# Third stage of a four-layer convolution net: group statistics back to rows through TensorE in two 12-bit halves, residual shared anew

## The chip, the cores and the metric

The kernel runs on one core of one Trainium2 chip. The metric is the time of one execution on the device in microseconds (us), the median of several runs. Inputs are random normal numbers of 8192 x 8 x 16 x 16 in float32.

## The reference, cut to what matters

Four layers, each with its input normalised by groups (four groups of two channels, over all pixels of a group of one sample) and added to its output:

```
def _gn(v, G=4, eps=1e-5):          # per sample and group: (g - mean) / sqrt(var + eps)
x = x + tensor_train_matvec(_gn(x)) + bias                 # layer 0
x = x + relu(batchnorm(conv3x3(_gn(x)) + bias))            # layer 1: statistics over the whole batch
x = x + conv3x3(round(clip(_gn(x) * sx)), qw) / (sx * sw) + bias   # layer 2: sx = 127 / max|_gn(x)|, over the whole batch
x = x + conv3x3(pad_edge(_gn(x)), sign(w) * mean|w|) + bias        # layer 3
```

The two maxima and averages over the whole batch cut the program into three stages. The third does layers 2 and 3, and the change is in it.

## The kernel before, in words

The batch is cut into 64 tiles of 128 samples. In the third stage a tile is an array of 128 partitions (channel and image row) by 2048 columns (sample and image column). A convolution along the rows and channels is a product with a band matrix of 128 x 128; the three taps along the columns are three products that add up in PSUM. A normalisation needs its group's mean and 1/sigma for each sample. Sums come out of TensorE with samples spread over the rows; to be used, they must lie along the columns again, the same in all partitions of a group ("rows").

Each step of a tile is a small function, and the table OPS names it. For tile i:

- "rows2", "spread2": 1/sigma times sx of the layer-2 normalisation, which stage 2 left in gnst as columns, is spread by DVE over a diagonal pattern (to_rows) and transposed by DVE in blocks of 32; TensorE then copies it to all partitions by a product with the selection matrix sel0, into r2 (bank ps_a).
- "v", "q": DVE multiplies the tile by r2 and rounds to int8, ACT turns it into bf16. "c2h1", "c2h0": layer 2's products, one half of the tile each, into pq.
- The residual: for half 0, ACT adds the bias ("bias") and DVE adds pq * inv ("stz", first2). For half 1, ACT makes pq * inv + bias ("z1"), and POOL adds it ("add1").
- "sq", "sums", "small", "pow": ACT squares, TensorE sums (s), DVE reduces and forms mean and variance, POOL takes the power -1/2.
- "rows3", "spread3": mean/sigma, 1/sigma and the mean of layer 2's input go the same way through to_rows, one transpose, and products with sel1 (into r3) and corr (into o3), a matrix that also takes the layer-2 mean out through the convolution's row sums.
- "t", "hi", "lo", "edl": DVE multiplies by r3; ACT and POOL split the product into two parts that float32r holds exactly. "c3h1a" to "c3h0b": layer 3's products into pf. "c", "corr": ACT and POOL add the offset o3. "out1", "out0": DVE adds pf, and SP stores the tile.

The order is written by hand: PHASE gives each step a time within a pipeline, tile i is shifted by PERIOD * i, and the sorted list is the order in which every engine's queue is filled. InOrder keeps that order on PE, DVE, ACT and POOL; a queue never overtakes. pq and pf share one PSUM pool of two buffers (tag "pc"), which rotate in the order in which the steps are written.

Of the kernel before, what the change touches and what calls it, by code (L numbers as in the profile page):

```python
# [8 lines left out]
F32 = mybir.dt.float32  # L9
F32R = mybir.dt.float32r  # L10
# [3 lines left out]
ALU = mybir.AluOpType  # L14
# [18 lines left out]
class InOrder:  # L33
# [5 lines left out]
    def __getattr__(self, name):  # L39
        op = getattr(self.engine, name)  # L40

        def call(*args, **kwargs):
# [2 lines left out]

PERIOD = 11.539
PHASE = {"rows2": 0, "spread2": 0.01, "v": 5.1, "q": 10.2, "bias": 10.4, "c2h1": 11.6, "z1": 13.1, "c2h0": 16.1, "add1": 17.1,
         "stz": 23.1, "sq": 24, "sums": 31.8, "small": 34.7, "pow": 37.3, "rows3": 42.7, "spread3": 45.3, "t": 46.3,  # L50
         "hi": 49.9, "c": 51.2, "lo": 51.9, "corr": 58.8, "edl": 60.3, "c3h0a": 60.4, "c3h0b": 61.3, "out0": 66.8,
         "c3h1a": 69.3, "c3h1b": 69.4, "out1": 69.41}

PACK0 = [("c0", R * C), ("c1", R * H), ("core2", 2 * R * W), ("bias0", W)]
# [5 lines left out]
def tile_net(ctx: ExitStack, tc: tile.TileContext, xb, xt_in, pack0, pack1, pack2, out):  # L62
# [33 lines left out]
    T2 = [dict() for _ in range(NT)]  # L96

    LATE = 5 if NT >= KEEP + STAY + 3 else 0

    def load2(i, what="yx"):  # L100
        for k in what:
# [45 lines left out]
    def late_constants(late):  # L147
# [101 lines left out]
        quarter = L["quarter"] = blocks(32, 1.0, "quarter")  # L249
        gpad = L["gpad"] = const.tile([P, NQ, 32], F32, name="gpad")  # L250
        dve.memset(gpad, 0.0)
        dve.tensor_copy(gpad[:, :, 0:G], quarter.unsqueeze(1).to_broadcast([P, NQ, G]))
        for k, name in enumerate(("sel0", "sel1", "corr")):

            t = L[name] = const.tile([P, CH], F32, name=name)
            dve.tensor_copy(t.rearrange("p (g n) -> p g n", g=G),
                            mod32[:, G * k:G * k + G].unsqueeze(2).to_broadcast([P, G, CH // G]))
        yield "statistics"

    def diagonal(n):  # L260
        ts = []
        for k in range(2):
            t = const.tile([P, NQ, 32], F32, name=f"diag_{n}_{k}")
            nc.gpsimd.memset(t, 0.0)
            ts.append(t)
        return ts
# [8 lines left out]
    def samples(t):  # L275
        return t.rearrange("p (b w) -> p b w", w=W)
# [422 lines left out]
    def put_quarter(ps):  # L699
        nc.vector.tensor_copy(ps[:, 0:NQ], L["quarter"])  # L700

    def stats_small(mv, st, ps, name):

        s = small.tile([P, 32], F32, name=f"s_{name}", tag="s")
        dve.tensor_reduce(s, samples(ps), AX.X, ALU.add)
        dve.transpose(st, s)
        sq = small.tile([P, G], F32, name=f"sq_{name}", tag="sqm")
        dve.tensor_copy(mv[:, 0:G], st[:, 0:G])
        dve.tensor_tensor(sq, st[:, 0:G], mv[:, 0:G], ALU.mult)
        dve.scalar_tensor_tensor(mv[:, G:2 * G], st[:, G:2 * G], EPS, sq, ALU.add, ALU.subtract)  # L710

    def stats_pow(mv):
        pool.tensor_tensor(mv[:, G:2 * G], mv[:, G:2 * G], mhalf[:, :G], ALU.pow)

    def to_rows(diag, mask, cols, name):

        at = 0
        for c in cols:
            n = c.shape[1]
            dve.tensor_tensor(diag[:, :, at:at + n], c.unsqueeze(1).to_broadcast([P, NQ, n]),  # L720
                              mask.unsqueeze(2).to_broadcast([P, NQ, n]), ALU.mult)
            at += n
        rows = small.tile([P, P], F32, name=f"rows_{name}", tag="rows")
        dve.transpose(rows, diag.rearrange("p q j -> p (q j)"))
        return rows
# [6 lines left out]
    with tc.tile_pool(name="p2", bufs=2) as p2, tc.tile_pool(name="ps2", bufs=2, space=PSUM) as ps2:  # L732
# [30 lines left out]

        def stats2(i):

            st, mv = psc[:, 32 + 32 * (i % 2):64 + 32 * (i % 2)], gnst[:, order2[i]]
            red = small.tile([P, 32], F32, name=f"s_c{i}", tag="s")
            dve.tensor_reduce(red, samples(T[i].pop("ps")), AX.X, ALU.add)
            dve.transpose(st, red)
            T[i]["sq"] = small.tile([P, G], F32, name=f"sq_c{i}", tag="sqm")  # L770
            act.copy(mv[:, 0:G], st[:, 0:G])
            act.activation(T[i]["sq"], st[:, 0:G], AF.Square)

        def sigma2(i):
            st, mv = psc[:, 32 + 32 * (i % 2):64 + 32 * (i % 2)], gnst[:, order2[i]]
            dve.scalar_tensor_tensor(mv[:, G:2 * G], st[:, G:2 * G], EPS, T[i].pop("sq"), ALU.add, ALU.subtract)
            stats_pow(mv)

        def spread2(i):
            T[i]["gb"] = ps = ps2.tile([P, BANK], F32, name=f"gb_{i}", tag="gb")  # L780
            rows = to_rows(diag[i % 2], mask2, [gnst[:, order2[i]]], f"c{i}")
            if i % 4 == 0:
                T[i]["gr"] = ps2.tile([P, 4, P], F32, name=f"gr_{i}", tag="gr")
                T[i]["top"] = p2.tile([P, 4, P], F32, name=f"top_{i}", tag="top")
            else:
                T[i]["gr"], T[i]["top"] = T[i - 1]["gr"], T[i - 1]["top"]
            for dst, sel in ((ps[:, 0:P], L["sel0"]), (T[i]["gr"][:, i % 4], L["sel1"])):
                pe.matmul(dst, sel, rows, start=True, stop=True)
# [60 lines left out]
    gm = const.tile([P, 1], F32, name="gm")  # L849
    nc.vector.tensor_reduce(pm, amax, AX.X, ALU.max)  # L850
    nc.gpsimd.partition_all_reduce(gm, pm, P, bass_isa.ReduceOp.max)
    nc.vector.reciprocal(sx, gm)
    nc.vector.tensor_scalar(sx, sx, 127.0, None, ALU.mult)
    nc.vector.tensor_tensor(inv, sx, L["sw"], ALU.mult)
# [6 lines left out]


    with ExitStack() as s:
        wk = s.enter_context(tc.tile_pool(name="wk3", bufs=2))
        ps_c = s.enter_context(tc.tile_pool(name="ps_c3", bufs=2, space=PSUM))
        ps_s = s.enter_context(tc.tile_pool(name="ps_s3", bufs=1, space=PSUM))
        order = [*kept, *(t for t in range(NT) if t not in kept)]

        sq3, t3, z3 = sqs[0], [sqs[1], xh], [y_stay[3][:, h * F // 2:(h + 1) * F // 2] for h in range(2)]
        T = [dict() for _ in range(NT)]  # L870
        AHEAD = min(NT, KEEP - 6)
        diag2, diag3 = diagonal("d"), diagonal("e")

        ps_a, ps_r, ps_o = (ps_s.tile([P, BANK], F32, name=f"ps_{n}", tag=n) for n in ("a", "r", "o"))
        r2, r3, o3 = ps_a[:, 0:P], ps_r[:, 0:P], ps_o[:, 0:P]
        put_quarter(ps_a[:, P:2 * P])
        mask, st3 = ps_a[:, P:P + NQ], ps_a[:, P + 32:P + 64]

        def load3(i):
            t = order[i]  # L880
# [6 lines left out]
        def halves(t):  # L887
            return t.rearrange("p (h n) -> p h n", h=2)

        def rows2(i):  # L890
            T[i]["rows2"] = to_rows(diag2[i % 2], mask, [gnst[:, order[i], G:2 * G]], f"d{i}")

        def rows3(i):
            mv = T[i].pop("mv")
            mr = small.tile([P, G], F32, name=f"mr_{i}", tag="mr")
            dve.tensor_tensor(mr, st3[:, 0:G], mv[:, G:2 * G], ALU.mult)
            T[i]["rows3"] = to_rows(diag3[i % 2], mask, [mr, mv[:, G:2 * G], gnst[:, order[i], 0:G]], f"e{i}")


        def spread2(i):  # L900
            pe.matmul(r2, L["sel0"], T[i].pop("rows2"), start=True, stop=True)

        def spread3(i):
            rows = T[i].pop("rows3")
            pe.matmul(r3, L["sel1"], rows, start=True, stop=True)
            pe.matmul(o3, L["corr"], rows, start=True, stop=True)

        def scale2(i):

# [9 lines left out]
            T[i]["q"] = q  # L919

        def bias2(i):
            x = halves(T[i]["x"])[:, 0]
            act.activation(x, x, AF.Identity, bias=L["bias2"], scale=1.0)

        def layer2(i, h):
# [8 lines left out]
        def first2(i):  # L934
            x = halves(T[i]["x"])[:, 0]
            dve.scalar_tensor_tensor(x, T[i].pop(("pq", 0)), inv, x, ALU.mult, ALU.add)

        def second2(i):
            act.activation(z3[i % 2], T[i].pop(("pq", 1)), AF.Identity, bias=L["bias2"], scale=inv)

        def add2(i):
            x = halves(T[i]["x"])[:, 1]
            pool.tensor_tensor(x, x, z3[i % 2], ALU.add)

        def square3(i):
            act.activation(sq3, T[i]["x"], AF.Square)
# [3 lines left out]
            sums_pe(T[i]["ps"], T[i]["x"], sq3)  # L950

        def stats3(i):
            T[i]["mv"] = small.tile([P, 2 * G], F32, name=f"mv3_{i}", tag="mv")
            stats_small(T[i]["mv"], st3, T[i].pop("ps"), f"d{i}")

        def pow3(i):
            stats_pow(T[i]["mv"])

        def offset3(i):
            T[i]["c"] = small.tile([P, P], F32, name=f"c_{i}", tag="c")  # L960
# [41 lines left out]
        def finish(i, h):  # L1002
# [4 lines left out]
            if T[i]["done"] == 2:  # L1007
                nc.sync.dma_start(out[order[i]], T[i]["x"])
                T[i].clear()

        OPS = {"rows2": rows2, "spread2": spread2, "v": scale2, "q": round2, "bias": bias2,
               "c2h0": lambda i: layer2(i, 0), "stz": first2, "c2h1": lambda i: layer2(i, 1), "z1": second2, "add1": add2,
               "sq": square3, "sums": sums3, "small": stats3, "pow": pow3, "rows3": rows3, "spread3": spread3, "c": offset3,
               "t": scale3, "hi": high3, "lo": low3, "corr": add3, "edl": edges3,
               "c3h0a": lambda i: layer3(i, 0, 0), "c3h0b": lambda i: layer3(i, 0, 1), "out0": lambda i: finish(i, 0),
               "c3h1a": lambda i: layer3(i, 1, 0), "c3h1b": lambda i: layer3(i, 1, 1), "out1": lambda i: finish(i, 1)}
        todo = [(op, i) for _, op, i in sorted((PERIOD * i + at, op, i) for op, at in PHASE.items() for i in range(NT))]
        for i in range(AHEAD):
            load3(i)
        for op, i in todo:  # L1020
            if op == "rows2" and AHEAD <= i + 4 < NT:
                load3(i + 4)
            OPS[op](i)

# [68 lines left out]
```

## Time and profile before

| | |
|---|---|
| Median of 3 runs | 3823.76 us (3823.36 to 3825.31) |
| Profiled execution, its own time | 3824.58 us |
| Its span | 3822.8 us |
| Busy over the span: PE, DVE, ACT, POOL | 94%, 89%, 66%, 80% |
| Third stage within it | 3064 to 3822.8 us |
| Period of a tile there, steady part | 11.47 us |

The span is from the first to the last instruction in the profile. PE is TensorE, PEld its weight loads, DVE the vector engine, ACT the scalar engine, POOL GpSimd, SP the queue that issues most transfers. Names such as ps_r, ps_o and ps_a are tiles of the program: r3 lies in ps_r, o3 in ps_o, r2 in ps_a. Nearly all instructions carry line 43, that of the helper InOrder, so they are told apart by their tiles.

### The profile page before, as it was taken

To read this page: it belongs to the slowest core of one execution; us is meant where nothing else is said; L and a number is where in the kernel's file an instruction comes from. 1 tells how busy PE (TensorE), PEld (TensorE's weight loads), DVE (VectorE), ACT (ScalarE), POOL (GpSimd) and SP (SyncE) were. 2 spreads that over 40 slices of the span, in tenths; PEclk is the share of its full clock that TensorE was granted. 3 is DMA by queue.
4 is the path that set the end of the run, shared out by engine and by line. 5 is a ranking of instruction groups with operands and counts; after the bars stand their busy time and mean duration, and the time that the engine had idled before them with its cause. 6 is when DMAs were issued, how large, how long until landed. Compare 5 with 4: busy or idle time off the path is not lost.

```text
span 3822.8 us, 52777 instructions
## 1 busy us (share of the span) xinstructions
PE 3598.8 (94%) x16264; PEld 2127.1 (56%) x16326; DVE 3386.0 (89%) x6313; ACT 2518.2 (66%) x2676; POOL 3048.8 (80%) x3104
## 2 busy tenths in 40 slices
PE   8999999999999999999999999997665589999999
PEld 4666666666666666666666666663221145555555
DVE  8988888888888888888888888877998889999997
ACT  5666666666666666666666666665665578778775
POOL 4877777778777777787777777865887779999998
PEclk9999999999999999999999999998776689999999
DMA  5787787878877878878788878766999724444442
GB/s 212 254 270 256 258 269 252 265 258 258 271 253 261 272 253 262 262 250 272 254 263 270 257 258 265 253 200 253 419 424 424 326 90 186 182 183 187 181 161 110
DMA packets 210809, 960.93 MB, mean 251 GB/s; under 512 B 44896, under 2 KB 45152, under 8 KB 110048
## 3 DMA queue, kind: packets, MB, share of 16 engines
q1 hardware_dynamic: 173808, 692.22, 48.8%
q0 software_dynamic: 36288, 264.26, 23.5%
q8 instruction: 131, 2.15, 0.2%
q14 instruction: 150, 1.23, 0.1%
q10 hardware_dynamic: 432, 1.08, 0.1%
HBM read 578.84 MB, written 378.54 MB: 250 GB/s over the span
## 4 chain that ended last, share of the span: by engine, by line
PE 85%; DVE 6%; DMA 4%; issue 2%; POOL 1%; ACT 1%; POOLq 0%; SPq 0%; DVEq 0%; ACTq 0%
PE po L43 45%; PE pu L43 12%; PE pf L43 10%; PE pm L43 6%; PE pq L43 4%; PE s L43 3%; PE pc L43 3%; DVE top L43 3%; PE ps_r L43 1%; DMA ys<-x_d 1%; DMA x_d<-u 1%; DMA x_d<-ys 1%; DMA u<-x_d 1%; DMA x_d<-xs 1%; DMA sq<-y_d 1%
## 5 line engine op out<-in xcount | busy, mean ns | idle before, releaser
L43 PE MATMUL po<-u,core 128*128 128x512 f32 (+1 forms) x4112 | 1844.7, 591 | 0.0
L43 ACT COPY u<-pu 128x2048 f32<-128x2048 f32 x512 | 955.4, 1866 | 512.9 <-PE pu L43 512.8
L43 PEld LDWEIGHTS po<-u,core 128*128 128x128 f32 x4112 | 744.6, 190 | 737.0 <-issue 736.1
L43 PE MATMUL pu<-core2r,xl 128*128 128x256 f32 x4032 | 678.6, 310 | 4.5 <-ACT u L43 3.5
L43 PEld LDWEIGHTS pu<-core2r,xl 128*128 128x128 f32 x4032 | 527.9, 189 | 127.9 <-issue 123.1
L43 POOL TENSOR_TENSOR bs<-bs,xh 128x512 fp32r<-128x512 f32 (+1 forms) x253 | 325.1, 1285 | 203.0 <-ACT xh L43 203.0
L43 POOL TENSOR_TENSOR v<-e 128x128 f32<-128x128 f32 x750 | 396.7, 540 | 0.0
L43 DVE TENSOR_TENSOR xs<-po,xs 128x512 f32<-128x512 f32 x256 | 176.9, 691 | 218.8 <-PE po L43 218.6
L43 ACT ACTIVATE m<-pm,b 128x128 f32<-128x128 f32 x250 | 91.7, 367 | 395.3 <-PE pm L43 395.3
L43 PEld LDWEIGHTS pm<-v,fast 128*128 128x128 f32 x2000 | 262.5, 192 | 119.7 <-issue 105.7
L43 POOL TENSOR_TENSOR e<-x1n,x 128x512 f32<-128x512 f32 x250 | 305.9, 1223 | 23.2 <-ACT x L43 15.8
L43 DVE TENSOR_TENSOR bs<-bs,stat 128x1024 f32<-128x1024 f32 x252 | 290.6, 1215 | 2.1
L43 POOL TENSOR_TENSOR xs<-xs,w 128x2048 f32<-128x2048 f32 x64 | 291.4, 4552 | 0.6 <-DMA xs<-in_xt 0.6
L43 PE MATMUL pm<-v,fast 128*128 128x128 f32 x2000 | 263.6, 275 | 0.0
L43 ACT ACTIVATE x<-x1n 128x512 f32<-128x512 f32 x500 | 247.0, 545 | 7.6 <-DVE x1n L43 7.6
L43 POOL TENSOR_TENSOR mv<-mv,mhalf 128x4 f32<-128x4 f32 x127 | 130.8, 1030 | 135.9 <-DVE mv L43 135.9
L43 PE MATMUL pf<-hi,sign 128*128 128x512 f32 x768 | 231.1, 439 | 0.0
L43 POOL DMA_DIRECT2D xl<-limb_d x252 | 149.8, 594 | 101.3 <-ACT x L43 38.4
L43 PE MATMUL pf<-lo,sign 128*128 128x512 f32 x768 | 218.0, 422 | 0.3 <-ACT lo L43 0.3
L43 POOL TENSOR_TENSOR v<-r 128x128 f32<-128x128 f32 x500 | 215.2, 447 | 0.0
L43 ACT ACTIVATE sq<-xs 128x2048 f32<-128x2048 f32 x103 | 197.0, 1913 | 18.2 <-DVE xs L43 13.6
L43 PE MATMUL gb<-rows_c,sel 128*128 128x128 f32 x128 | 40.8, 413 | 166.3 <-DVE rows_c L43 166.3
(308 smaller groups left out, 7195.3 us busy)
## 6 DMA issues: line engine op xcount, KB each, us to landing
xl<-limb_d POOLq DMA_DIRECT2D x252, 1024.0 KB, 7.4
x_d<-xs SPq DMA_DIRECT2D x76, 1024.0 KB, 8.4
xs<-in_xt SPq DMA_DIRECT2D x64, 1024.0 KB, 7.6
bs<-in_xb SPq DMA_DIRECT2D x63, 1024.0 KB, 5.6
limb_d<-xh SPq DMA_DIRECT2D x1008, 64.0 KB, 4.4
limb_d<-bs SPq DMA_DIRECT2D x1008, 64.0 KB, 5.2
y_d<-ys SPq DMA_DIRECT2D x60, 1024.0 KB, 8.0
u<-x_d SPq DMA_DIRECT2D x34, 1024.0 KB, 6.5
```

Of the source, the lines that this page charges most:

```text
L43: return self.tc.keep_in_program_order(op(*args, **kwargs))
```

## The change

Four things change in the third stage:

1. The way back to rows. The diagonals and DVE's two transposes go. Four columns of four values (mean/sigma and 1/sigma of tile i, mean of layer 2's input of tile i, and 1/sigma of tile i + 4 for layer 2) are put together by ACT ("cols") and DVE ("mr"); ACT rounds them to float32r ("lhh"), DVE takes the rest ("lhl"). One float32r product with the identity turns all 32 columns into 32 rows ("turn"), ACT copies them out of PSUM ("rows"), and four float32r products of 32 rows ("spread") copy them to all partitions: back2 to r2 for tile i + 4, back3 to r3, and corr in two parts to o3. Tiles -4 to -1 have these steps alone. The constants for them are made between the stages.
2. The squared mean is made by ACT ("sqm"), between DVE's "small" and "var".
3. The residual of half 1: DVE takes 384 of its 1024 columns ("stz1"), with the bias for them in "bias"; "z1" and "add1" keep 640.
4. PERIOD and all of PHASE are new, and the tiles' load is issued beside "v" instead of "rows2". In stage 2 only the place at which gnst is written changes.

```diff
-PERIOD = 11.539
-PHASE = {"rows2": 0, "spread2": 0.01, "v": 5.1, "q": 10.2, "bias": 10.4, "c2h1": 11.6, "z1": 13.1, "c2h0": 16.1, "add1": 17.1,
-         "stz": 23.1, "sq": 24, "sums": 31.8, "small": 34.7, "pow": 37.3, "rows3": 42.7, "spread3": 45.3, "t": 46.3,
-         "hi": 49.9, "c": 51.2, "lo": 51.9, "corr": 58.8, "edl": 60.3, "c3h0a": 60.4, "c3h0b": 61.3, "out0": 66.8,
-         "c3h1a": 69.3, "c3h1b": 69.4, "out1": 69.41}
+PERIOD = 11.2
+PHASE = {"v": 0, "q": 2.2, "bias": 7.9, "c2h1": 9.5, "stz1": 11.3, "c2h0": 11.4, "z1": 11.7, "stz": 12.6, "add1": 13.6,
+         "sq": 14.5, "sums": 21.2, "small": 23, "cols": 23.01, "sqm": 23.1, "var": 23.6, "pow": 26.3, "mr": 29.7, "lhh": 32,
+         "lhl": 34, "turn": 34.5, "rows": 34.7, "spread": 34.9, "t": 35, "hi": 37, "c": 43.8, "lo": 46.2, "edl": 47.1,
+         "c3h1a": 48.4, "corr": 51.1, "c3h1b": 53.1, "out1": 56, "c3h0a": 57, "c3h0b": 57.3, "out0": 57.5}
+LEAD = 4
+SHARE = 24
...
+        def columns3(i):
+            T3[i] = col = wk.tile([P, 4 * G], F32, name=f"col_{i}", tag="col", bufs=4)
+            if i < 0:
+                for k in range(2):
+                    act.copy(col[:, 2 * G * k:2 * G * k + 2 * G], gnst[:, i + LEAD])
+            elif i + LEAD < NT:
+                act.copy(col[:, 2 * G:3 * G], gnst[:, i, 0:G])
+                act.copy(col[:, 3 * G:], gnst[:, i + LEAD, G:2 * G])
+            else:
+                act.copy(col[:, 2 * G:], gnst[:, i])
...
+        def shift3(i):
+            if i >= 0:
+                dve.tensor_tensor(column(i, 0), st3[:, 0:G], column(i, 1), ALU.mult)
+        def high_column3(i):
+            act.copy(lhs[i % 2][:, 0:4 * G], T3[i])
+        def low_column3(i):
+            lh = lhs[i % 2]
+            dve.tensor_tensor(lh[:, 4 * G:], T3.pop(i), lh[:, 0:4 * G].bitcast(F32), ALU.subtract)
+        def turn3(i):
+            pe.matmul(turned, lhs[i % 2], identr, start=True, stop=True)
         def rows3(i):
-            mv = T[i].pop("mv")
-            mr = small.tile([P, G], F32, name=f"mr_{i}", tag="mr")
-            dve.tensor_tensor(mr, st3[:, 0:G], mv[:, G:2 * G], ALU.mult)
-            T[i]["rows3"] = to_rows(diag3[i % 2], mask, [mr, mv[:, G:2 * G], gnst[:, order[i], 0:G]], f"e{i}")
-        def spread2(i):
-            pe.matmul(r2, L["sel0"], T[i].pop("rows2"), start=True, stop=True)
+            T3["rows", i] = rows = wk.tile([K3, P], F32R, name=f"rows_{i}", tag="rows")
+            act.copy(rows, turned)
         def spread3(i):
-            rows = T[i].pop("rows3")
-            pe.matmul(r3, L["sel1"], rows, start=True, stop=True)
-            pe.matmul(o3, L["corr"], rows, start=True, stop=True)
+            rows = T3.pop(("rows", i))
+            if i + LEAD < NT:
+                pe.matmul(r2, back2, rows, start=True, stop=True)
+            if i >= 0:
+                pe.matmul(r3, back3, rows, start=True, stop=True)
+                for k, part in enumerate((high, low)):
+                    pe.matmul(o3, part, rows, start=(k == 0), stop=(k == 1))
...
+        def third2(i):
+            x = halves(T[i]["x"])[:, 1][:, 0:SHARE * W]
+            dve.scalar_tensor_tensor(x, T[i]["pq", 1][:, 0:SHARE * W], inv, x, ALU.mult, ALU.add)
...
+        def square_mean3(i):
+            T[i]["sqm"] = small.tile([P, G], F32, name=f"sqm_{i}", tag="sqm")
+            act.activation(T[i]["sqm"], st3[:, 0:G], AF.Square)
+        def variance3(i):
+            dve.scalar_tensor_tensor(column(i, 1), st3[:, G:2 * G], EPS, T[i].pop("sqm"), ALU.add, ALU.subtract)
...
-        todo = [(op, i) for _, op, i in sorted((PERIOD * i + at, op, i) for op, at in PHASE.items() for i in range(NT))]
+        SHARED = ("cols", "mr", "lhh", "lhl", "turn", "rows", "spread")
+        todo = [(op, i) for _, op, i in sorted((PERIOD * i + at, op, i) for op, at in PHASE.items()
+                                              for i in range(-LEAD if op in SHARED else 0, NT))]
```

## The prediction

> **What bounds the kernel now.** I read the slices first, then the stretch in which the third stage is steady, then the chain of waits there. In the stretch table the columns are time, busy us of PE, PEld, DVE, ACT and POOL (with counts), granted clock, DMA share and GB/s.
>
> ```profile
> 3400.00:3500.00 100.00, 99.53 (x502) 58.35 (x510) 92.26 (x170) 79.25 (x71) 98.36 (x35) 1.00 0.49 188
> ```
>
> PE and POOL are both full and DVE nearly so, so busy shares don't decide. The chain does; columns are start, length, what:
>
> ```profile
> 3394.64 1.30 PE pq L43 x6
> 3395.94 6.15 PE pf L43 x24
> 3402.09 0.66 PE pq L43 x3
> 3402.75 0.05 issue
> 3402.80 0.60 PE pq L43 x2
> 3403.40 1.85 PE s L43 x16
> 3405.25 0.42 PE ps_r L43 x2
> 3405.67 0.22 PE ps_o L43 x2
> 3405.89 0.22 PE ps_a L43 x2
> 3406.12 1.30 PE pq L43 x6
> ```
>
> One tile takes 11.47 us (3394.64 to 3406.12) and all of it is PE: pq 2.61, pf 6.15, sums 1.85, and 0.86 for the three row products. Does PE lose time to DVE in it? The timeline says the weight load of ps_r waited for DVE, both in the steady part and in the drain:
>
> ```profile
> 3405.18 0.30 PEld L43 LDWEIGHTS ps_r<-rows_e,sel 128*128 128x128 f32 x2 [0.84 <-DVE rows_d L43]
> ...
> 3772.32 0.30 PEld L43 LDWEIGHTS ps_r<-rows_e,sel 128*128 128x128 f32 x2 [0.84 <-DVE xs L43]
> ```
>
> The second has no rows_d in front of it (that tile's rows ended 1.8 us earlier) and the same 0.84. So the gap is PE's own, after the sums. PE is the bound, DVE and POOL lie just below it.
>
> The gap recurs where the first stage goes in and out of 32-row products:
>
> ```profile
> 36.27 0.19 PEld L43 LDWEIGHTS po<-u,core 128*128 128x128 f32 x1 [0.24 <-issue]
> 37.22 0.74 PEld L43 LDWEIGHTS pu<-w,ys 32*128 32x128 f32 x16 [0.76 <-ACT xh L43]
> 38.30 0.30 PEld L43 LDWEIGHTS po<-u,core 128*128 128x128 f32 x2 [0.33 <-issue]
> ```
>
> A po product is 0.43 and starts with the load of the next, so the last begins at 36.70 and streams to 37.13; the next po begins 0.11 after its load, at 38.41. Of those 1.28 us the pu products stream 0.85 (16 passes of 256 columns at 0.213, four side by side). Going in and out costs about 0.43: in 0.12, out 0.25, rest unexplained.
>
> **What the Trainium skill says.** "TensorEngine Tiling (Array Packing)", Key Properties: changing the tiling mode drains the engine. The trace agrees: 0.43 here; around the sums (32 columns) 1.85 - 4 x 0.427 = 0.14, and ps_r's 0.42 - 0.22 = 0.20, together 0.34. "TensorE: Matmul & The Clock Gate", LDWEIGHTS: a load costs by columns, not rows, P/1.2 ns: 107 ns for 128 columns, 27 for 32. The trace has 0.11 from load to load among ps_r, ps_o, ps_a, and 1.03 for eight single-pass products of 256 columns, 0.13 each. "PSUM — Partial Sum Buffer", rule 2: float32r products force the full column group. No run shows yet whether this spares the drain for a 32-column one.
>
> **The change, part by part.**
>
> *PE.* Out: 0.86. In: the turn (32 weight columns, 128 streamed), and four single-pass products with 32 contraction rows. The four: into the row tiling 0.12; four starts 0.107 apart (weight loads, 3 x 0.107) and 0.053 of streaming = 0.37; out 0.25; total 0.74. Bounds: 0.22 (four times 0.053, no drains) to 0.85. The turn: 0.10 if columns are forced full, 0.06 to 0.44 else (in 0.12, 0.08, out 0.24); I take 0.10. After the sums now comes c2h0, whose bf16 weights load in 0.10 where f32 took 0.19: 0.15 instead of 0.20. PE's tile: 2.61 + 6.15 + 1.85 + 0.15 + 0.10 + 0.74 = **11.60**, against 11.47.
>
> *DVE.* Out: two transposes 0.62, four diag 0.66, copy and square 0.32: 1.60. In: stz1 on 384 columns (1.243 less 640 x 1.04 ns = 0.58) and lhl 0.16. Net, DVE loses 0.86 of its 10.6 a tile (92.26% of 11.47), but var now waits for ACT's sqm, about 0.5 (0.05 to ACT, 0.18, 0.05 back, and small's tail): covered, since t waits for the spread longer.
>
> *ACT.* Two copies, square, lhh, rows: each 0.16 to 0.22, overlapping to about 0.06 to 0.1 (second stage: copy 3041.38, square 3041.43, next 3041.50); bias grows by 384 x 0.833 ns = 0.32 and z1 shrinks as much. ACT goes from 9.1 (79.25% of 11.47) to about 9.6 of 11.6. Covered.
>
> *POOL.* lo 4.28 + corr 3.70 + add1 2.42 + pow 1.03 = 11.43; add1 falls to 640 columns, 1.53. POOL 10.5: no longer near the bound.
>
> *Waits.* Path a: v, stz1, lhl, turn, c3h0, spread, t, out0, mr, out1, v. DVE from t to lhl's end 2.26 + 1.16 + 0.17 + 1.2 + 2.26 + 0.5 + 0.16 = 7.7; lhl to t's start 0.1 + 0.2 + 3.06 + 0.12 + 0.11 + 0.27 = 3.86. Sum 11.5. Path b over two tiles: 7.98 to t's start, t 2.34, hi 2.03, lo 4.37, add1 1.53, pow 0.98, corr 3.8: 23.0, 11.5 a tile. Both lie 0.1 below PE. Where c3h0b comes after the spread they are 1.5 (b: 0.8) shorter.
>
> *New waits, in an ordinary tile.* With tile i in the turn, the sort gives PE the order c2h1, sums, c2h0, turn, c3h0a, c3h0b, spread, c3h1a, c3h1b and DVE mr, out1, v, stz1, lhl, small, var, stz, t, out0. Counting from c3h1b's end: out1 0.3, v 1.5, stz1 3.8, lhl to 4.46, so the turn may start at 4.56, and PE comes to it at 4.61 (1.3 + 1.85 + 0.15 + 1.31): no loss, but only 0.05 to spare; all of c3h0 is queued behind. On ACT sqm waits for small (5.5) and holds up rows (to 6.05), q (to 7.9), edl (8.4) and sq (10.2); spread wants rows at 6.24 or 7.77, c3h1b wants edl at 10.0, the sums sq at 12.9: no loss. The spread also waits for v, which is still to be read from r2: v ends at 3.8. c3h1a waits for stz: 7.2 against 8.5. out1 waits for corr on POOL: 11.65 against 11.9 in the next tile.
>
> *Orders.* The written order is a sort on sums, and three pairs tie: 34.9 and 57.3 - 22.4 (spread, c3h0b); 35 and 12.6 + 22.4 (t, stz); 0 and 56 - 56 (v, out1). Rounding breaks them tile by tile. Evaluating the sort: t comes before stz for tiles 23, 24, 28, 29, 33, 34, 38, 39 (spread ahead of c3h0b) and 48, 53, 58 (behind). c3h1a takes over the PSUM buffer that stz reads, two being in rotation. So PE then waits for spread, t and stz. On the same clock, spread ahead: the turn 4.61, c3h0a to 6.24, ps_r's product 6.47, t 6.74 to 9.0, stz to 10.24, c3h1a 10.4; it could start at 8.5, when c3h0b is done: **1.9 lost**. Spread behind: t from 8.27, stz to 11.77, c3h1a 11.9: **3.4 lost**. 8 x 1.9 + 3 x 3.4 = 25.4. Queued behind the held c3h1a: c3h1b, the next c2h1 and sums, all of PE. In six tiles v precedes out1, and c2h0 waits for out1's buffer about 0.5: +2, with the first two in the fill.
>
> *Ends.* The stage takes 3064.2 (gm) to 3822.8 = 758.6, of which 64 x 11.47 = 734.1, ends 24.5. The nominal depth falls from 69.4 to 57.5, but the first periods last 5.7 (3076.7, 3082.5, 3088.2: ACT-bound with little on PE), ACT has more to do in them, and v(0) waits for six short steps where two were (estimate +1). I take -2, with -11.9 (all the depth) and +3 as bounds. Constants before it hide in the 0.55 that DVE waits for gm. No DMA is added; the load tied to rows2 is tied to v, at the same phase.
>
> Sum: about 58 steady tiles x 0.13 = +7.5; +25.4; +2; -2: **+33**. The profiled execution had 3824.6 (span 3822.8), 0.8 above the median 3823.8. Against it: 3857.
>
> **The rivals.**
> 1. *No drains around the four products*: 0.43 for them, so PE's tile 11.29; path a at about 11.4 binds where the spread is late. 58 x -0.09 = -5, and the swaps 26, v 2, ends -2: +21, 3845. For: no single-pass product of 32 rows is in the trace. Against: the f32 ones show the drain.
> 2. *The turn drains as well*: PE 11.95, 58 x 0.48 = 28 + 25 + 2 - 2: +53, 3877. For: sums do it. Against: the forced full columns.
> 3. *Not slower: the five products cost array time alone.* Place: turn and spread on PE. Price: 5 x 0.056 = 0.28 for 0.86, PE 10.89; 58 x -0.58 = -34. The stalls then put the other engines ahead, so PE's own time may count after them; +25 + 2, and the depth comes whole, -12: -19; with path a holding back some 7, 3812. It decides from a PE tile of 11.2 (58 x 0.27 = 16 against 27 - 12). For: the shorter depth is real, and DVE and POOL are relieved. Against: weight loads of 128 columns show 0.11 apart everywhere.
> That the change doesn't do what it says can be only in the share for POOL, which costs nothing either way now.
>
> **Numbers.** 0.2% (7.6 us) is about what a measurement of this kernel can tell from no change. The main case has 0.47 (3842 to 3872 by its bounds), rival 1 0.22, rival 2 0.10, rival 3 0.21 (two thirds faster, a third same). With a little of rival 1 in "same": faster 0.14, same 0.09, slower 0.77. Range 3818 to 3878: it leaves out about 0.13 below and 0.05 above.
>
> **What would show it.** The chain after: PE pieces of 11.6 a tile, about 0.7 to 0.8 between the pf of c3h0b and of c3h1a. Right if steady tiles lie at 11.5 to 11.7 and tiles 23 to 39 and 48, 53, 58 show PE idle 2 to 3.5 before a pf, released by DVE (stz). Rival 1: 0.45 there. POOL's share falls to about 91%, DVE to about 84% (9.7 of 11.6). Wrong if the pf after a swapped pair starts without a wait, or if the steady tile is below 11.3.

## The result: slower by 3.3%

| | before | after |
|---|---|---|
| Median | 3823.56 us (3822.62 to 3825.31, 4 runs) | 3948.54 us (3947.57 to 3951.47, 4 runs) |
| Span of the profiled execution | 3822.8 us | 3949.3 us |
| Ratio after/before | | 1.0328, interval 1.031 to 1.0345 |

All of it arises in the third stage, which begins at 3064 us in both. DVE's "small" begins with one reduction per tile (`s_d<-s` before, `s<-s` after), and from one to the next is the period of a tile. By it the 126.5 us between the two spans part as follows:

| | before | after | difference |
|---|---|---|---|
| span's start to the first reduction | 3081.4 | 3084.7 | +3.3 |
| first four periods | 37.8 | 43.8 | +6.1 |
| the other 59 periods | 673.3 | 780.5 | +107.2 |
| last reduction to the end | 30.3 | 40.3 | +10.0 |

The plain period went from 11.47 to 12.71 us. The tiles with a swapped order (t ahead of stz; the spread comes ahead of c3h0b, "early", or behind it, "late") cost about 33 above that: four pairs with an early spread 4.4 each, three tiles with a late spread 5.4, 5.2 and 4.6. What is left of the 107.2, 74 over 59 tiles, is 1.25 per tile: the plain period again. So some three fifths of the loss lie in tiles for which the prediction saw no loss but TensorE's own 0.13.

### The profile after, in the same views

The stretches, with the columns of before: time, busy us of PE, PEld, DVE, ACT and POOL, clock, DMA share, GB/s. The first holds no swapped tile, the second holds some.

```profile
3200.00:3300.00 100.00, 94.11 (x446) 50.91 (x452) 85.44 (x103) 75.42 (x105) 83.56 (x32) 1.00 0.44 169
...
3400.00:3500.00 100.00, 90.25 (x411) 49.10 (x417) 78.17 (x97) 70.08 (x93) 76.83 (x29) 0.98 0.38 148
```

PE is no longer full even where no tile is swapped, and nothing else is: POOL fell from 98 to 84, DVE from 92 to 85. When every engine has gaps at an even period, a loop of waits sets the period. The chain of waits names it (start, length, what):

```profile
3415.53 2.35 DVE xh L43 x2
...
3421.45 1.21 DVE v L43
3422.66 0.53 DVE xk L43
3423.19 1.15 DVE lh L43
...
3424.47 0.22 PE ps_o L43
3424.70 3.12 PE pf L43 x12
3427.81 0.25 PE ps_a L43
3428.06 0.13 PE ps_r L43
...
3428.21 2.35 DVE sq L43 x2
```

From t (`xh`, 3415.53) to the next t (`sq`, 3428.21) are 12.68 us: t, then out0 and out1 in the gap of this quotation, v, stz1 (`xk`), **lhl (`lh`), 1.15**, the turn, c3h0, the spread's first two products. It is path a of the prediction, which came to 11.5 there. One link has another size: lhl was put at 0.16. The timeline shows why; its columns are start, length, engine and instruction, and in brackets the idle time before it and who ended that.

```profile
3417.97 1.92 ACT L43 CAST hi<-xh 128x2048 fp32r<-128x2048 f32 x1 [1.34 <-DVE xh L43]
...
3420.02 4.27 POOL L43 TENSOR_TENSOR lo<-xh,hi 128x2048 fp32r<-128x2048 f32 x1 [2.02 <-ACT hi L43]
...
3423.10 1.22 DVE L43 TENSOR_TENSOR lh<-col,lh 128x16 fp32r<-128x16 f32 x1
```

POOL's lo runs until 3424.29, and lhl, an instruction on 16 columns, starts at 3423.10 and ends at 3424.32. It ends with lo. The 64 instances that belong to tiles (lowest, median and highest ns; the four of the tiles -4 to -1 take 0.16 to 0.18 us):

```profile
L43 DVE TENSOR_TENSOR lh<-col,lh x64: 160/1218/3730, 3091.9 to 3919.3; 128x16 fp32r<-128x16 f32 x64
```

Where POOL is between two instructions it takes the 160 ns that the prediction had. "SBUF — State Buffer", section "Who interferes with whom", of the Trainium skill says that a DVE instruction with two inputs in SBUF shares a read port with GpSimd, and that whoever comes second waits for the whole of the other's instruction. The trace agrees: lhl reads `col` and `lh`, both in SBUF, and each of the 48 longer ones ends 0.03 to 0.04 us after a lo. The diag instructions of the kernel before, which have the same shape and take 0.16, read their mask from PSUM.

So what sets the period isn't DVE's work ahead of lhl, though the chain goes through it: started beside lo, lhl ends when lo ends, however early it starts. The loop is t, hi, lo, the end of lhl, turn, c3h0, spread and the next t: 8.79 us from t's start to lhl's end (3415.53 to 3424.32) and 3.89 from there to the next t. Where the spread is early, c3h0b's 1.5 us drop out of this loop, and such tiles have a period of 11.66 where nothing is swapped (the next one 13.4).

In the drain it happens twice nearly in full. lhl takes 3.72 beside a lo from 3904.82 and 3.73 beside a lo from 3918.77, both in the chain of waits: 2 x 3.56 = 7.1 of the tail's 10.0 us. The rest is TensorE behind these two waits: its 12 pf products take 4.49 and 4.71 us instead of 3.15 (from 3909.49 and 3923.50), at a granted clock of 0.62 and 0.60.

A swapped tile looks as predicted. c3h1a (`pf<-hi`) comes to its turn and waits for stz (`u<-pq`), which stands behind t:

```profile
3399.56 2.35 DVE L43 TENSOR_TENSOR sq<-u,ps_r 128x1024 f32<-128x1024 f32 x2 [1.81 <-PE ps_r L43]
3401.83 1.28 DVE L43 SCALAR_TENSOR_TENSOR u<-pq,inv,u 128x1024 f32<-128x1024 f32 x1
3403.25 1.80 PE L43 MATMUL pf<-hi,sign 128*128 128x512 f32 x6 [1.76 <-DVE u L43]
```

PE idles 1.76 there; 1.9 was forecast for the early spread. With a late spread it idles 3.51 in each of the three tiles, and 3.4 was forecast. What makes these tiles longer still stands behind the wait, in the chain:

```profile
3723.74 5.47 PE pf L43 x12
```

The same 12 products take 3.36 us from 3403.25, at a granted clock of 1.00. In the three late tiles they take 5.47, 5.30 and 4.69, at 0.50, 0.54 and 0.64. That is 2.1, 1.9 and 1.3 us of the 5.4, 5.2 and 4.6.

### The profile page after: what moved, and what is told of

It is laid out like the page before. It is cut to its first block, busy times and chain, and to the rows that moved or that the text cites. A ratio compares the mean times of both kernels' runs of the same rounds, so it can differ in the third digit from the quotient of the medians.

```text
span 3949.3 us, 52753 instructions
## 1 busy us (share of the span) xinstructions
PE 3645.9 (92%) x16204; PEld 2117.5 (54%) x16266; DVE 3401.6 (86%) x5936; ACT 2550.3 (65%) x3010; POOL 2995.5 (76%) x3100
## 4 chain that ended last, share of the span: by engine, by line
PE 72%; DVE 17%; DMA 6%; issue 3%; ACT 1%; POOL 1%; SPq 0%; DVEq 0%; POOLq 0%; ACTq 0%
PE po L43 43%; PE pu L43 12%; PE pf L43 7%; PE pm L43 6%; PE pc L43 3%; DVE v L43 2%; DVE top L43 2%; DVE sq L43 2%; DVE u L43 2%; DVE xh L43 2%; DVE xs L43 2%; DVE lh L43 1%; DVE ys L43 1%; DMA x_d<-u 1%; DMA u<-x_d 1%
## 5 line engine op out<-in xcount | busy, mean ns | idle before, releaser
L43 PE MATMUL pf<-lo,sign 128*128 128x512 f32 x768 | 229.8, 438 | 0.8 <-ACT lo L43 0.8
L43 PE MATMUL pq<-q,band 128*128 128x480 bf16 (+1 forms) x706 | 188.0, 387 | 14.5 <-ACT q L43 5.3
L43 POOL TENSOR_TENSOR lo<-sq,hi 128x2048 fp32r<-128x2048 f32 x32 | 136.5, 4267 | 79.5 <-ACT hi L43 79.5
```

Of the source, the lines that this page charges most:

```text
L43: return self.tc.keep_in_program_order(op(*args, **kwargs))
```

## The experiments

My theory after this reading: lhl's wait for POOL makes the plain tile 12.7, and the swaps make the 33. Each is taken away by itself first, then the rest is taken apart. Ratios are against the kernel before, run on the same chip (3823.4 to 3824.0).

| kernel | us | ratio (interval) | plain tile, us |
|---|---|---|---|
| e1: lhl reads the rounded part from PSUM | 3922.21 | 1.0259 (1.0243 to 1.0274) | 12.40 |
| e2: stz ahead of t | 3914.92 | 1.0236 (1.0219 to 1.0253) | 12.71 |
| e3: whole-array products | 3938.83 | 1.0301 (1.0286 to 1.0317) | 12.61 |
| e4: before, mask in SBUF | 4170.73 | 1.0908 (1.0891 to 1.0924) | 17.07 |
| e5: e1 + e2 + z1 first | 3878.27 | 1.0140 (1.0125 to 1.0156) | 12.32; 11.67 with early spread |
| e6: e5 + whole array | 3868.88 | 1.0117 (1.0103 to 1.0131) | 12.2; 11.40 with early spread |
| e7: e6 + spread always early | 3830.49 | 1.0018 (1.0011 to 1.0024) | 11.40 |
| e8: e5 + spread always early | 3845.64 | 1.0057 (1.0043 to 1.0071) | 11.67 |
| e9: after, the orders alone | 3897.94 | 1.0196 (1.0182 to 1.0210) | 12.40 |
| e10: before, row products later | 3829.21 | 1.0014 (1.0007 to 1.0020) | 11.44 |
| e11: e9 + z1 first | 3930.38 | 1.0282 (1.0265 to 1.0299) | 13.00 |
| e12: before + the share behind out1 | 3931.33 | 1.0282 (1.0266 to 1.0297) | 13.13 |
| e13: before + the share ahead of t | 3829.31 | 1.0014 (1.0008 to 1.0021) | 11.47 |

### e1: lhl's second input from PSUM

```diff
         def high_column3(i):
             act.copy(lhs[i % 2][:, 0:4 * G], T3[i])
+            act.copy(high_ps[i % 2], lhs[i % 2][:, 0:4 * G].bitcast(F32))
...
-            dve.tensor_tensor(lh[:, 4 * G:], T3.pop(i), lh[:, 0:4 * G].bitcast(F32), ALU.subtract)
+            dve.tensor_tensor(lh[:, 4 * G:], T3.pop(i), high_ps[i % 2], ALU.subtract)
```

> The changed kernel, but lhl reads the rounded part from PSUM (ACT copies it there as well), so it has one operand in SBUF instead of two. Theory 1 (lhl's second SBUF operand makes it wait for the instruction that POOL is running, and this closes the loop t, hi, lo, lhl, turn, c3h0, spread, t at 12.7 us): lhl takes 0.16 to 0.2 for every tile, the plain tile falls from 12.71 to PE's own time of about 12.05, the swapped tiles stay as they are; 3948.5 - 0.65 x 55 = about 3912. Theory 2 (lhl is long by its float32r output or its narrow strided form): lhl stays at 1.2 and the time at 3948. Theory 3 (the drains around turn and spread make PE the bound at 12.7, lhl only fills a gap): lhl 0.16, time unchanged within 8.

Measured: 3922.21, tile 12.40. lhl (`lh<-col,ps_r`) takes 0.16 in all 68 places, so the cause of its length is shown: the float32r output and the 16 columns are as before. The tail falls from 40.3 to 34.0 us. But the plain tile lost only 0.31, and theory 1 said 0.65. The next wait is one that the prediction doesn't have, in the chain of waits of e1:

```profile
3411.86 0.62 DVE xk L43
...
3412.50 0.89 ACT bs L43
...
3413.44 3.33 PE pf L43 x12
```

c3h0 (`pf`) waits for z1 (`bs`), and z1 for stz1 (`xk`). z1 reads 640 columns of pq and stz1 the other 384, so no value passes between them, but they read one buffer in PSUM. "PSUM — Partial Sum Buffer", section "PSUM bank collisions raise a hardware error", says that the compiler's scheduler puts a dependency between two engines' accesses to one bank and quadrant, reads too. This program does have ACT wait for DVE there, and the trace shows ACT starting 0.02 after DVE's end. (In the program pq is two banks of 512 columns, and 384 lies inside the first. Whether a split at 512 would go without the wait was not tried.)

### e2: the swaps taken out

`"stz": 12.6` becomes `12.55`: the tie of these two is gone, and stz comes ahead of t in every tile.

> The changed kernel with stz at 12.55 instead of 12.6, so that stz is ahead of t in every tile; nothing else. Theory of the swaps (c3h1a waits for spread, t and stz where t is ahead): the waits of 2 to 5 us of a pf for DVE go, four pairs give 4.4 each and three single tiles 4.6 to 5.4 each, together 33: about 3916. Rival (the long tiles come from where the spread stands relative to c3h0b, and the swap only goes with it): 3948 within 5.

Measured: 3914.92, 33.6 us less than after, and the former late-spread tiles run at 12.71. The swaps are worth what was read off the periods, and 25.4 was forecast. The slower clock behind them goes as well: it stays at 1.00 from 3110 to 3870.

### e3: do the products of 32 rows drain TensorE?

The columns are widened with zeros to 128, so turn and spread use the whole array.

```diff
-    K3 = 8 * G
+    K3 = P
```

> The changed kernel with the turn and the row products on the whole array: the 32 columns and 32 rows are filled with zeros to 128, so the number of products and their streamed columns stay. Theory 1: the drains go (about 0.35 around turn and spread on the loop), the plain tile goes from 12.71 to about 12.35, 55 x 0.36 = 20: 3929; the pf after a spread starts 0.45 after the spread's first load instead of 0.58 to 0.69; lhl stays at 1.2. Theory 3 (drains make PE the bound): the plain tile falls by all of PE's saving, to 11.4 to 11.6, about 3880.

Measured: 3938.83, tile 12.61, less gained than either theory said. lhl has grown to 1.29: it ends with lo, so whatever comes sooner ahead of it is waited away. What is left is what lies between lhl's end and the next t: the spread's first product falls from 0.25 to 0.06, and the turn rises from 0.22 to 0.30. The way out of the spread lies behind t's start and not in this loop. The question waits for a kernel in which TensorE is the bound (e7, e8).

### e4: the port in the kernel before

```diff
-        mask, st3 = ps_a[:, P:P + NQ], ps_a[:, P + 32:P + 64]
+        mask, st3 = L["quarter"], ps_a[:, P + 32:P + 64]
```

> The kernel before the change with one edit: the mask of the diagonals is read from its SBUF original instead of its copy in PSUM, so that the four diag products have two SBUF operands. No float32r output is in them. Theory 1 (two SBUF operands wait for POOL): diag_e starts while POOL runs lo and waits for its end, 2.2 us (lo ends at 3404.87 where diag_e starts at 3402.7), and others behind corr; at least 2.2 a tile, 3824 + 140 = 3965 or more. Theory 2: 3824 within 8.

Measured: 4170.73. The groups of the steady part (count, busy us and mean ns, idle before) show instructions that took 160 to 170 ns with their mask in PSUM:

```profile
L43 DVE TENSOR_TENSOR diag_e<-gnst,quarter 128x16 f32<-128x16 f32 x38 | 90.0, 2368 | 0.0
...
L43 DVE TENSOR_TENSOR diag_e<-mr,quarter 128x16 f32<-128x16 f32 x38 | 45.6, 1200 | 1.3
```

The third, on `mv`, has a mean of 1565. In the timeline it runs beside corr, to the same end:

```profile
3505.32 3.72 DVE L43 TENSOR_TENSOR diag_e<-mv,quarter 128x16 f32<-128x16 f32 x1
3505.32 3.68 POOL L43 TENSOR_TENSOR u<-u,c 128x2048 f32<-128x2048 f32 x1
```

One word in the kernel before costs 347 us. All 125 diag instructions longer than 0.2 us end within 0.05 us of the end of a POOL instruction: it is the same cause as lhl's, made in a kernel without the change. The wait isn't all of the 347. Of 5.6 us more per tile, the three diag_e have some 4.6; behind them ps_a and pq take 0.79 and 2.56 us instead of 0.22 and 1.30 (from 3511.12), in a stretch whose granted clock was 0.70 (3509 to 3514; 1.00 in the kernel before).

### e5, e6: z1 ahead of stz1

e5 is e1 and e2 with `"z1": 11.25` (11.7 before), so that stz1 waits for z1. e6 adds e3's whole array.

> The changed kernel with three edits: lhl reads the rounded part from PSUM (as in the first run), stz ahead of t (as in the second), and z1 at 11.25 instead of 11.7, ahead of stz1, so that ACT need not wait for DVE's share of the same PSUM buffer. Theory A (with lhl short, the plain tile was held at 12.40 by c3h0a waiting for z1, which waits for stz1 because both read one PSUM buffer): z1 starts before v has ended, and the plain tile falls to PE's own 12.05 (drains around turn and spread included); 3922 - 34 (swaps) - 0.33 x 59 = about 3868. Theory B (something else holds 12.40): swaps alone, about 3888.

> The kernel of e5_z1_first, and the turn and row products on the whole array (filled with zeros to 128). Theory A: PE's own tile falls to about 11.3, and the path v, stz1, lhl, turn, c3h0a, c3h0b, spread, t binds at 11.4 to 11.5; 3868 - 0.6 x 60 = about 3832. Theory B (drains cost nothing on PE): as e5_z1_first.

Measured: 3878.27 and 3868.88, both slower than forecast. Turning the pair round makes lhl wait with stz1 behind z1, and tiles whose spread comes behind c3h0b stay at 12.32 (e6: 12.2). In e5 DVE idles 0.58 us ahead of stz1 until z1 has ended. Only those with an early spread reach 11.67 and 11.40. A wait that is turned round isn't removed; what stands behind the second of the two is then late.

### e7, e8: the spread always ahead of c3h0b

Both take `"c3h0b": 57.35` and `"out1": 55.95`, so that out1 precedes v as well. e7 adds that to e6, e8 to e5.

> The kernel of e6, and the two other ties broken one way: the spread is ahead of c3h0b (57.35 for 57.3) and out1 ahead of v (55.95 for 56) in every tile. Theory A: the path through the spread is 1.5 shorter, so PE's own 11.3 binds: about 3820, within 0.3% of the kernel before the change. If PE's tile is 11.2 or less, it is faster than before, about 3812.

> The kernel of e5, and the two other ties broken as in e7, so that only the array's tiling is different from e7. Theory A: PE alone binds, and its tile with drains is seen clean: 2.61 + 6.15 + 1.85 + 0.15 + 0.48 (turn) + 0.83 (spread) = 12.07, so about 3868, like e5, and 0.75 x 63 = 47 more than e7. Theory B (drains are hidden): no more than 10 above e7.

Measured: 3830.49 and 3845.64. TensorE is the bound in both, with no wait in a tile, so they show what the new products cost. The chain of e8 (products of 32 rows) after sums and pq, which are 1.85 and 1.40 in both:

```profile
3405.45 0.06 PE ps_o L43
3405.51 1.60 PE pf L43 x6
3407.10 0.25 PE ps_a L43
3407.36 0.11 PE ps_r L43
3407.47 0.22 PE ps_o L43 x2
3407.69 4.86 PE pf L43 x18
```

and the same stretch in e7 (whole array):

```profile
3412.57 0.13 PE ps_o L43
3412.70 1.59 PE pf L43 x6
3414.29 0.06 PE ps_a L43
3414.35 0.12 PE ps_r L43
3414.46 0.22 PE ps_o L43 x2
3414.68 4.72 PE pf L43 x18
```

In and out of the row tiling cost 0.25 - 0.06 = 0.19 on the first product and 4.86 - 4.72 = 0.14 on the pf after the last; the turn of 32 weight columns costs nothing beyond itself (its pf is 1.60 against 1.59) and is 0.07 shorter than on the whole array (0.06 against 0.13). In sum the tile is 11.67 against 11.40. The two kernels are 15 us apart, between theory A's 47 and theory B's 10: e8's forecast was 22 too long, mostly because it gave the turn 0.48 where 0.06 was measured. e7 missed its 3820 by 10. e7 has a shorter tile than the kernel before and is yet 0.18% slower: its first reduction comes 3.3 us later, its first four periods are 4.7 us longer in sum (42.5 against 37.8), its tail 0.9, and the other 59 periods give back 3.3.

### e9, e11: which of the two waits holds the tile

e9 is the kernel after with the three order edits alone (stz 12.55, out1 55.95, c3h0b 57.35). e11 adds `"z1": 11.25`. Neither has the copy to PSUM.

> The changed kernel with nothing but the three ties broken one way in every tile (stz 12.55, out1 55.95, c3h0b 57.35): lhl still has two SBUF operands, z1 still comes after stz1. Theory A (the waits of lhl and z1 cost only through the path that also holds c3h0b; with the spread ahead of it that path is 1.5 shorter and PE's 11.67 binds, as in the single early tiles): 3846 to 3850, the same as e8. Theory B (the wait for POOL costs by itself): a plain tile stays above 12 and the time above 3870.

> The kernel after with all four orders of the kernel that reached 11.67 us a tile (z1 11.25, stz 12.55, out1 55.95, c3h0b 57.35), but lhl takes the rounded part from SBUF again. It parts the two causes of the 52 us between orders alone (3898) and that kernel (3846). Theory A (bank wait alone): with z1 ahead of stz1 the tile is 11.67 to 11.75, 3846 to 3852. Theory B (each of the two waits would do): at that rhythm lhl becomes ready at the very moment at which POOL goes from lo to add1 (lo ended at 3404.96, lhl started at 3404.97, add1 ran 3404.91 to 3406.47), so from SBUF it has to wait for add1's end, 1.36 us later; the turn has 0.18 to spare, so the tile is 12.4 to 12.9 and the time 3890 to 3925.

e9 measured: 3897.94, tile 12.40. Theory A falls, and the time is over the 3870 of theory B, but what holds the tile isn't lhl: by its new place it comes after lo has ended and takes 0.17, save in four tiles near the ends; the wait for the shared buffer remains and holds the tile by itself, as the timeline shows:

```profile
3400.97 0.88 ACT L43 ACTIVATE bs<-pq,bias,inv 128x640 f32<-128x640 f32 x1 [2.58 <-DVE xk L43]
3401.90 1.32 PEld L43 LDWEIGHTS pf<-hi,sign 128*128 128x128 f32 x6 [0.67 <-ACT bs L43]
```

The loop is TensorE from c3h0a to c3h1b, 7.26 us, and then out1, v, stz1 and z1 until the next c3h0a, 5.14: 12.40, with an early spread as with the late one of e1.

e11 measured: 3930.38, tile 13.00: theory B, and a little more than it said. With z1 out of the way lhl falls on add1:

```profile
3412.79 1.53 POOL L43 TENSOR_TENSOR xk<-xk,bs 128x640 f32<-128x640 f32 x1
3412.85 1.50 DVE L43 TENSOR_TENSOR lh<-col,lh 128x16 fp32r<-128x16 f32 x1
```

With e8 these are three kernels with the same three orders: neither wait 11.67; the port's alone (e11) 13.00; and e9, which has both in its program but meets the buffer's alone, 12.40. Each alone holds the tile above TensorE's 11.67, and they don't add up: with the buffer's wait taken out e9 becomes slower, since lhl then comes while add1 runs. A fourth kernel, e9 with lhl reading from PSUM, was not run. Since lhl waits for nothing in e9's ordinary tiles, I would expect 12.40 again; that isn't shown.

### e10: row products moved in the kernel before

`"spread2"` 0.063 and `"spread3"` 46.2178, so that c2h1 and not ps_r follows the sums.

> The kernel before the change with two phases altered (spread2 0.063, spread3 46.2178), so that PE makes the three row products after c2h1 and not right behind the sums. Theory A (PE is the bound; a product right behind the sums pays the change of tiling, 0.20 with f32 weights against 0.10 with bf16 weights, and behind c2h1 there is none): the tile goes from 11.47 to about 11.37, 0.1 x 60 = 6: about 3818. Rival (DVE or POOL lie so close below PE that they bind): 3824 or more.

Measured: 3829.21, not faster. The tile is 11.44: ps_r falls from 0.42 to 0.22, but pq rises by 0.10 and pf by 0.06. The exit after the sums is paid by whoever comes next, at about half as much when that is a bf16 product. The fill is longer (first reduction at 3086.1, first four periods 41.0 against 37.8), which outweighs it.

### e12, e13: the share of the residual alone

The kernel before, with 384 columns of half 1 on DVE and no other part of the change.

```diff
+        def third2(i):
+            x = halves(T[i]["x"])[:, 1][:, 0:24 * W]
+            dve.scalar_tensor_tensor(x, T[i]["pq", 1][:, 0:24 * W], inv, x, ALU.mult, ALU.add)
```

e12 writes it behind out1 (13.15) and z1 leaves the release of pq to the end of the tile; e13 writes it ahead of t (11.65) and z1 releases pq as before.

> The kernel before with one part of the change alone: 384 of the 1024 columns of half 1's residual go from ACT and POOL to DVE (phase 13.15, behind z1 and so behind t and out1 in DVE's order). POOL's busy share falls from 98% to about 91%, DVE's rises from 92% to about 97%. Theory 1 (TensorE alone is the bound, as in the prediction: POOL's relief is worth nothing): the tile stays at 11.47, 3822 to 3828. Theory 2 (DVE's 0.58 us more reach TensorE, since rows_d ends only 0.8 us ahead of the product that needs it): tile up to 11.8, 3832 to 3845. Theory 3 (POOL's 98% held something): faster by over 5 us.

> Again the kernel before with the share of the residual alone, but with DVE's part (stz1, phase 11.65) written ahead of t, out1 and z1, so that layer 3's c3h0a takes over c2h1's buffer as in the kernel before and not the one that out1 still has to read (in the run before it waited for out1: 13.13 us a tile). By the trace of before c2h1 ends at 3407.36 and t starts at 3407.57: stz1 would end at 3408.1, z1 (which must follow it, since both read one buffer) at 3409.0 instead of 3409.26, c3h0a starts at 3410.33 and so does not wait. t comes 0.53 later. Theory 1 (TensorE alone is the bound; the share is worth nothing, and its bank wait costs only where c3h0a stands right behind it): tile 11.47, 3822 to 3828. Theory 2 (DVE's 0.53 reaches TensorE through v, q or rows_d): tile 11.6 to 12.0, 3832 to 3857. Theory 3 (POOL's 98% held something): under 3818.

e12 measured: 3931.33, tile 13.13, far off all three theories. c3h0a was given another buffer of the two, the one that out1 still had to read, and waited for it 59 times (out1, `xs<-pf`, runs from 3408.61 to 3409.89):

```profile
3409.94 1.80 PE L43 MATMUL pf<-hi,sign 128*128 128x512 f32 x6 [1.38 <-DVE xs L43]
```

So it says nothing on the share. Which buffer a product gets is settled when the program is built. Built with one difference from e13 at a time (built, not run), the place behind out1 moves c3h0a's buffer and the later release doesn't. So the two buffers are not simply handed out in turn, as the description of the kernel says: a reader written elsewhere can change who gets which. e13 measured: 3829.31, tile 11.47 as before, theory 1 for the tile:

```profile
3400.00:3500.00 100.00, 100.00 (x501) 59.32 (x503) 96.64 (x176) 80.31 (x71) 90.73 (x36) 1.00 0.48 186
```

POOL fell from 98 to 91, DVE rose from 92 to 97, and TensorE's period didn't move. In the kernel before, the share is worth nothing in the steady part and costs some 4 us in the fill: the first reduction comes at 3085.4 instead of 3081.4, and from there to the last are 711.7 us against 711.1. None of the thirteen beats the kernel before.

## Why the prediction was wrong, point by point

- **Direction**: right, and for the swapped orders (33 of the 125) by the forecast mechanism. **Size**: +33 forecast, +125 measured; most of the rest comes from a wait that it didn't have.
- **Failed step 1: "lhl 0.16" (under DVE, and in path a).** That is what a diag takes, which has the same shape but one input in PSUM. With both in SBUF it took 1.2 in plain tiles and up to 3.73, ending with lo. So "Waits" lacks a loop: by the prediction's own figures t 2.34, hi 2.03, lo 4.37 and 3.86 from lhl's end to the next t are 12.60, and 12.68 was measured, where paths a and b were put at 11.5, "0.1 below PE". The plain tile was 12.7 in place of the 11.6 forecast: +1.1 on some 58 tiles, about 64 us, the largest single error. e1 and e4 show the cause.
- **Failed step 2: "New waits, in an ordinary tile ... no loss".** It went through who needs whose values and missed who shares a buffer. z1 waits for stz1, and c3h0a for z1: 12.40 by itself (e1, e9). On the prediction's own clock stz1 ends at 4.3, so z1 behind it (0.9 measured) would have put c3h0a at 5.2 instead of 4.7; in e9 it comes 5.14 after c3h1b's end. In the kernel after it lies hidden behind the first error, so mending that alone gave 26 us and not the 64 that it had cost.
- **Failed term: "Ends", -2 within -12 to +3.** About +14 measured: a tail of +10.0 (7.1 lhl, 2.9 the slower clock behind it), +3.3 ahead of the first reduction, and 1.1 by which the first four periods grew beyond four plain ones. In e13 the share alone puts the first reduction 4.0 later; that the 3.3 of the kernel after have the same cause was not tried.
- **TensorE's tile, 11.60**: right, 11.67 where nothing waits (e8). The four products with in and out came to 0.25 + 0.11 + 0.22 + 0.14 = 0.72 against 0.74. The exit of the sums onto pq was 0.10 (0.15 forecast), the turn 0.06 (0.10). pf itself is 6.3 without the way out (6.31 in e7) instead of 6.15, which I can't assign. So the sum agrees to 0.07 partly because 0.11 too much and 0.17 too little offset each other. And since the tile wasn't TensorE's, the number decided nothing.
- **Orders, 25.4 and 2**: mechanism, tiles and stalls right (1.76 and 3.51 us of idle TensorE for 1.9 and 3.4), about 33 measured (e2: 33.6). The late-spread tiles cost about 5 because the pf behind the stall runs 1.3 to 2.1 us longer at a granted clock of 0.50 to 0.64, for which the prediction has no term. The early pairs cost 2.2 a tile; what a slower clock has in that (0.86 from 3390 to 3395) was not separated, nor were the 2 us for v ahead of out1.
- **Rival 1 and 3 (no drains)**: fall with e7 and e8. The row tiling costs 0.27 a tile, and even without it the tile is 11.40, not 11.29 or the 11.2 from which rival 3 decided. **Rival 2 (the turn drains)**: falls too.
- **What would show it**: POOL 91% and DVE 84% of an 11.6 tile are 10.6 and 9.7 us. POOL's 83.56% of 12.71 is 10.6. DVE's 85.44% is 10.9. Of the 1.1 more, 0.9 is lhl waiting, which the profile books as busy; in e1 DVE has 9.9.

## What to carry to other kernels

Price an instruction by where its operands lie, not only by its shape: a row with one input in PSUM says nothing on the same row with two in SBUF while GpSimd runs. When work on a PSUM buffer is shared out to a second engine, count the two readers as one queue and ask who stands behind the second. An instruction that ends when another engine's ends belongs into that engine's loop, so add the loop up from there. And where a path lies 0.1 us below the bound, its small links decide the forecast, so each deserves its bounds from both sides.

## What the runs showed of the hardware that I had not expected

- DVE's wait for GpSimd is for the whole instruction however small its own is: 16 columns waited 3.72 us beside corr's 3.68 (e4), and GpSimd's lo kept its length (median 4.28 before and in e4, 4.27 after).
- Such waiting counts as busy in the profile. It shows as a spread of durations within one group (160/1218/3730 ns) and as an end that falls together with one of GpSimd's, so a group's lowest, median and highest are worth a look.
- A wait can cost more than its length. Behind 3.51 us of idle TensorE the next 12 pf took 4.69 to 5.47 us instead of 3.36, at a granted clock of 0.50 to 0.64; in e2, without these waits, the clock stayed at 1.00.
- The 32-column float32r turn (`128*32`) left no mark on the product behind it (1.60 against 1.59 us), while 32-row products cost 0.19 going in and 0.14 going out. The Trainium skill, "TensorEngine Tiling (Array Packing)", Key Properties, has a change of mode drain the engine without a number; the rows agree, the turn doesn't show it.
